# Another order in front of the first attention turn of a decoder layer

## The chip, the cores and the metric

The kernel runs on one core of a Trainium2 chip. The metric is the device time of one execution in microseconds (us), as the median over runs. The engines are named as the profile names them: PE (TensorE, with PEld for its weight loads), DVE (VectorE), ACT (ScalarE), POOL (GpSimd) and SP (the engine that issues most transfers). All data are float32.

## The reference, cut to what matters

One decoder layer over two sequences of 1024 tokens with 256 features: a linear attention with two decays per head, a cross attention to 154 context rows, and a mixture of eight experts (two per token) with a shared expert, each on a normalised input and added to the residual.

```python
x = x + linear_attn(layernorm(x), w_qkv, w_out, alpha, beta)
x = x + cross_attn(layernorm(x), ctx, weights, mask, Wq, bq, Wk, bk, Wv, bv, Wo, bo)
x = x + experts(layernorm(x), ...)

def linear_attn(x, w_qkv, w_out, alpha, beta):      # 16 heads of 16
    q, k, v = split(x @ w_qkv, 3)
    q, k = elu(q) + 1, elu(k) + 1
    for d in (sigmoid(alpha), sigmoid(beta)):       # one decay per head
        run_kv, run_k = scan(d, k * v), scan(d, k)  # out[t] = d * out[t-1] + in[t]
        den = max(sum(q * run_k over the head), 1e-6)
        outs.append(q * run_kv / den)
    return concat(outs) @ w_out

def cross_attn(x, ctx, weights, mask, ...):         # 16 heads of 64
    q, k, v = x @ Wq + bq, ctx @ Wk + bk, ctx @ Wv + bv
    att = softmax(where(mask, -inf, (q @ k.T) / 8 * weights))
    return (att @ v) @ Wo + bo
```

## The kernel before

Tokens are cut into four blocks of 512 (`BLK`), two per sequence; a block is four tiles of 128 tokens. The cross attention runs in 64 "turns" (block, group of four heads, tile). A turn takes `score` (L1007, PE), `weigh` (L1016, DVE), `hide` (L1028, DVE), `power` (L1037, ACT), `divide` (L1044 on DVE, L1045 and L1048 on POOL) and, three turns later, transposes (L961) and the product with the values. Behind the turns come the router, the shared expert and the routed experts.

In front of the first turn stands a prologue, which is written out by hand: inside `manual_schedule` every engine gets its instructions in the order in which Python emits them, and each engine works its own queue strictly in that order, waiting on semaphores. Later work (the linear attention of blocks 1 to 3, the rest of the keys and values, the norms of blocks 2 and 3) is cut into generators, `linear_rest`, `rest_of_kv` and `other_norms`, of which every turn takes one piece (`ahead`).

The prologue does these things, each with its lines:

- `load_x`, and the weight loads on SP's queue in the order alpha_beta, w_qkv, x of block 1, ctxT, bk, Wk, Wv, w_out, x of blocks 2 and 3, and then the rest.
- `layernorm_early` for blocks 0 and 1: statistics on DVE (L186, L187), the reciprocal root on POOL (L190, L191), the normalised rows on DVE for block 0 (L199) and on ACT for block 1 (L204), eight transposes on PE (L212), and copies out of PSUM (L216 on DVE, L218 on ACT).
- `make_decay`: the decays of alpha and beta, spread over the partitions by four small matmuls (L358), copied out on DVE (L362).
- The linear attention of block 0, for two chunks c of 128 features: `make` projects k or q (`project`, L451), ACT takes an exponential and a Relu of it (L463, L464), and DVE joins them (the "map", L466). `make_v` multiplies v into k (L473). `scan_k` and `scan_kv` are decayed prefix sums on DVE (L478, two decays f per chunk), of keys and of keys times values. `times_q` (L490) and `num_q` (L497) multiply by q. `sum_rows` sums per head on PE with `sel` (L505), and DVE takes the reciprocal (L513, L514). `spread` brings it back over the partitions with `selT` (L524), DVE multiplies (L533), and `result` multiplies by w_out (L543) and adds to x (L548).
- `keys(o)` makes one eighth of the keys of the cross attention (L378, and L382 on ACT), `vals` half of the values of a sequence (L390, L395), `rests` the values of the last 26 context rows (L402, L406).
- The norm of the queries of block 0 in two halves (`layernorm`, L228 to L256), `add_bo` on POOL (L608), and the first three pieces of block 1 (`second`).

The maps and the multiplications by PSUM results are put off in two lists, `mapped` and `later`, and issued together by `take_later`. PSUM has three tiles `mm` of one bank, one `tp`, and two tiles `sc` of two banks, which the scores use; in the prologue every product goes to an `mm` tile. A float32 matmul shows as two records in the trace, so a projection has four records.

Before, the prologue makes keys 0 to 3 and the values of sequence 0, and `rest_of_kv` takes keys 4 and 5 in the first turn and keys 6 and 7 in the fourth.

Of the kernel before, what the change touches and what calls it, by code (L numbers as in the profile page):

```python
# [8 lines left out]
F32 = mybir.dt.float32  # L9
# [16 lines left out]
def tile_decoder_layer(  # L26
# [81 lines left out]
    def load_x(blk, parts=1):  # L108
        b, r = divmod(blk, NBB)
        n = TPB // parts  # L110
        for i in range(parts):
# [3 lines left out]
                in_=x[b, q0 : q0 + n * P, :].rearrange("(t p) d -> p t d", p=P),  # L115
            )

    load_x(0, 2)

    Wq_sb = xconst.tile([P, ND, NO * P], F32, tag="Wq", name="Wq_sb")  # L120
# [53 lines left out]
    for e in range(E):  # L174
        nc.gpsimd.memset(rank[:, e : e + 1], float(E - e))

    def layernorm_early(blk, lnT):

        src = xr[blk]
        first = blk == 0  # L180
        st = small.tile([P, TPB, 6], F32, tag="st", name="st")
        mv = small.tile([P, TPB, 2], F32, tag="mv", name="mv")
        rstd = small.tile([P, TPB], F32, tag="rstd", name="rstd")
        nmr = small.tile([P, TPB], F32, tag="nmr", name="nmr")
        for t in range(TPB):
            nc.vector.bn_stats(st[:, t, :], src[:, t, :])  # L186
            nc.vector.bn_aggr(mv[:, t, :], st[:, t, :])  # L187
            if t == 1:
                yield
        nc.gpsimd.tensor_scalar(rstd, mv[:, :, 1], LN_EPS, None, ALU.add)  # L190
        nc.gpsimd.tensor_tensor(rstd, rstd, half[:, 0:1].to_broadcast([P, TPB]), ALU.pow)  # L191
        if not first:
            nc.gpsimd.tensor_tensor(nmr, mv[:, :, 0], rstd, ALU.mult)
            nc.gpsimd.tensor_scalar(nmr, nmr, -1.0, None, ALU.mult)
        yield
        xn = xnp.tile([P, TPB, DX], F32, tag="xn", name="xn")
        for t in range(TPB):
            if first:
                nc.vector.tensor_scalar(  # L199
                    xn[:, t, :D], src[:, t, :], mv[:, t, 0:1], rstd[:, t : t + 1],  # L200
                    ALU.subtract, ALU.mult,
                )
            else:
                nc.scalar.activation(  # L204
                    xn[:, t, :D], src[:, t, :], AF.Identity,
                    bias=nmr[:, t : t + 1], scale=rstd[:, t : t + 1],
                )
        yield
        for c in range(ND):
            tp = mm_tile()  # L210
            for t in range(TPB):
                nc.tensor.transpose(  # L212
                    tp[:, t * P : (t + 1) * P], xn[:, t, c * P : (c + 1) * P], ident
                )
            if first and c == 0:
                nc.vector.tensor_copy(lnT[:, c, :], tp)  # L216
            else:
                nc.scalar.copy(lnT[:, c, :], tp)  # L218
        yield

    def layernorm(blk, lnT, xn, t0=0, nt=TPB):
# [62 lines left out]
    wk = weights.enter_context(tc.tile_pool(name="wk", bufs=1, side="right"))  # L284


    ab = kw.tile([NR, 1], F32, tag="ab", name="ab")
    nc.sync.dma_start(out=ab, in_=alpha_beta)
    wqkv_sb = kw.tile([P, ND, 3 * D], F32, tag="wqkv", name="wqkv_sb")
    nc.sync.dma_start(out=wqkv_sb, in_=w_qkv.rearrange("(c p) o -> p c o", p=P))  # L290
    load_x(1)
    ctxT_sb = wk.tile([P, ND, B * SK], F32, tag="ctxT", name="ctxT_sb")
    nc.sync.dma_start(out=ctxT_sb, in_=ctxT.rearrange("(c p) k -> p c k", p=P))
    nc.sync.dma_start(out=bk_sb, in_=bk)
    Wk_sb = wk.tile([P, ND, NO * P], F32, tag="Wk", name="Wk_sb")
    nc.sync.dma_start(out=Wk_sb, in_=Wk.rearrange("(c p) o -> p c o", p=P))
    Wv_sb = wk.tile([P, ND, H * DK], F32, tag="Wv", name="Wv_sb")
    nc.sync.dma_start(out=Wv_sb, in_=Wv.rearrange("(c p) o -> p c o", p=P))
    wout_sb = kw.tile([P, 2 * ND, D], F32, tag="wout", name="wout_sb")
    nc.sync.dma_start(out=wout_sb, in_=w_out.rearrange("(c p) o -> p c o", p=P))  # L300
# [66 lines left out]
    nbk = wk.tile([P, NO], F32, tag="nbk", name="nbk")  # L367

    def prepare_kv():
        for b in range(B):  # L370
            nc.gpsimd.tensor_copy(ctx2[:, :, b, :], ctxT_sb[:, :, b * SK + P : (b + 1) * SK])
        nc.gpsimd.memset(vr_sb, 0.0)
        nc.gpsimd.tensor_scalar(nbk, bk_sb, -1.0 / (MASKED * float(DK) ** 0.5), None, ALU.mult)

    def keys(o):
        ps = mm_tile()
        for c in range(ND):
            nc.tensor.matmul(  # L378
                ps[:, : B * SK], lhsT=Wk_sb[:, c, o * P : (o + 1) * P],
                rhs=ctxT_sb[:, c, :], start=(c == 0), stop=(c == ND - 1),  # L380
            )
        nc.scalar.activation(  # L382
            kT[:, o, :], ps[:, : B * SK], AF.Identity, bias=nbk[:, o : o + 1],
            scale=-1.0 / (MASKED * float(DK) ** 0.5),
        )
# [50 lines left out]
    class Linear:  # L436
# [8 lines left out]
            self.num = lp.tile([P, NX, BLK], F32, tag="num", name="num", bufs=1)  # L445
            self.rden = lp.tile([P, TQ], F32, tag="rden", name="rden", bufs=1)

        def project(self, o):
            ps = mm_tile()
            for c in range(ND):  # L450
                nc.tensor.matmul(  # L451
                    ps, lhsT=wqkv_sb[:, c, o * P : (o + 1) * P], rhs=lnTa[self.blk][:, c, :],
                    start=(c == 0), stop=(c == ND - 1),
                )
            return ps
# [10 lines left out]
                lambda: nc.vector.scalar_tensor_tensor(dst, e, 1.0, dst, ALU.min, ALU.add)  # L466
            )

        def make_v(self, c):

            ps = self.project(2 * ND + c)
            k = self.k[c]
            later.append(lambda: nc.vector.tensor_tensor(k, ps, k, ALU.mult))  # L473

# [40 lines left out]

            later.append(take)

        def spread(self, half):

            js = (2 * half, 2 * half + 1)  # L520
            pss = {j: mm_tile() for j in js}
            for xi in range(NX):
                for j in js:
                    nc.tensor.matmul(  # L524
                        pss[j][:, xi * TQ : (xi + 1) * TQ],
                        lhsT=selT[rows_of(j), xi * P : (xi + 1) * P], rhs=self.rden[rows_of(j), :],
                        start=True, stop=True,
                    )
            for j in js:
                n = self.num[:, :, j * TQ : (j + 1) * TQ]  # L530
                ps = pss[j].rearrange("p (x q) -> p x q", x=NX)
                later.append(
                    lambda n=n, ps=ps: nc.vector.tensor_tensor(n, ps, n, ALU.mult)  # L533
                )

        def result(self, t0):

            ps = mm_tile()
            po = ps.rearrange("p (t d) -> p t d", d=D)
            for i in range(2):  # L540
                at = (t0 + i) * P
# [49 lines left out]
    def take_later():  # L591
        for take in mapped + later:
            take()
        mapped.clear()
        later.clear()
# [27 lines left out]
    with region:  # L623
        L = [Linear(blk) for blk in range(NBLK)]
        a = L[0]
        second = L[1].pieces()
        dk = make_decay()
        make_selT(0)
        next(ln[0])
        next(ln[0])  # L630
        next(dk)
        next(ln[0])
        next(ln[1])
        next(ln[0])
        next(dk, None)
        next(ln[1])
        next(ln[1])
        make_sel()
        prepare_kv()
        a.make("k", 0)  # L640
        take_later()
        a.begin()
        a.make("q", 0)
        a.scan_k(0, 0)
        a.make_v(0)
        a.scan_k(0, 1)
        take_later()
        a.make("k", 1)
        a.make("q", 1)
        for f in range(2):  # L650
            a.scan_kv(0, f)
        next(ln[1])
        take_later()
        for f in range(2):
            a.times_q(0, f)
        a.make_v(1)
        for f in range(2):
            a.scan_k(1, f)
        keys(0)
        keys(1)  # L660
        take_later()
        for j in range(1, TG):
            make_selT(j)
        nc.gpsimd.memset(zero, 0.0)
        for f in range(2):
            a.times_q(1, f)
        vals(0, 0)
        a.sum_rows()
        for f in range(2):
            a.num_q(0, f)  # L670
        take_later()
        for f in range(2):
            a.scan_kv(1, f)
        rests(0)
        a.spread(0)
        for f in range(2):
            a.num_q(1, f)
        take_later()
        rests(512)
        a.spread(1)  # L680
        take_later()
        keys(2)
        next(ln[2])
        next(ln[2])
        a.result(0)
        a.result(2)
        half_0, half_2 = later
        later.clear()
        next(second)
        half_0()  # L690
        lnTq[0] = lnT_tile(0)
        xq = xnp.tile([P, TPB, DX], F32, tag="xn", name="xn")
        nq0 = [layernorm(0, lnTq[0], xq, t, 2) for t in (0, 2)]
        next(nq0[0])
        half_2()
        next(nq0[1])
        next(nq0[0])
        take_later()
        keys(3)
        next(second)  # L700
        for _ in range(ND):
            next(nq0[0])
        next(nq0[1])
        take_later()
        for _ in range(ND):
            next(nq0[1])
        add_bo(0)
        vals(0, 512)
        next(second)


    HL = HID - (NHC - 1) * P
# [195 lines left out]
    with bctx:  # L908
# [197 lines left out]

        def rest_of_kv():

            keys(4)
            keys(5)  # L1110
            yield
            for n0 in (0, 512):
                vals(1, n0)
                yield
            keys(6)
            keys(7)
            yield
            bias_rows()
            yield
# [463 lines left out]
```

## Time and profile before

| what | value |
|---|---|
| runs | 646.98, 645.94, 643.26 us; median 645.94 |
| profiled execution | 646.79 us, its span 645.1 us |
| mean granted clock of PE | 0.984 |
| busy: PE, DVE, ACT, POOL | 605.5, 431.9, 296.8, 244.0 us |
| first matmul record | 8.19 us |
| first turn (first L1016 on DVE) | 70.35 us |
| last turn (last L1016) | 385.0 us |

The span runs from the first to the last instruction of the one profiled execution. A row of the timeline has the start in us, the length in us, the engine, the line, the operation, the tiles written and read, their shapes, how many instructions are merged, and in brackets how long the engine had been idle before it and what ended that. A row of the windows has a stretch, its length, the busy time of PE, PEld, DVE, ACT and POOL with the number of records, the granted clock, the share of the transfer engines and GB/s.

### The profile page before, as it was taken

The page shows a single profiled execution, that of the slowest core. Times are in us where ns is not written, and L with a number is a line of the kernel's source. Part 1 is how long each engine was busy: PE and PEld are TensorE (multiplying, and loading weights), DVE is VectorE, ACT ScalarE, POOL GpSimd, SP SyncE. Part 2 cuts the span into 40 slices and gives each one's busy share as a digit, 9 for nine tenths or more (in the row PEclk, how much of TensorE's full clock was granted, in tenths as well). Part 3 has the DMA queues.
Part 4 walks back from the last instruction along what each step waited for, and adds up shares of the span by engine and source line. Part 5 has one row for each costly group of instructions (what it writes and reads, how often), then busy time and mean ns, then how long its engine had stood idle before and what let it go on. Part 6 is the DMA issues. An engine that isn't in the chain of part 4 may idle for free. (4 is left out here: it accounts for less than half of the span.)

```text
span 645.1 us, 10259 instructions
## 1 busy us (share of the span) xinstructions
PE 605.5 (94%) x3024; PEld 393.3 (61%) x3024; DVE 431.9 (67%) x1379; ACT 296.8 (46%) x894; POOL 244.0 (38%) x375
## 2 busy tenths in 40 slices
PE   4898999999999998999899989899899999999897
PEld 3354466555577545777467654667477777777644
DVE  4887595689844899656984694248456655556557
ACT  1512577677545766437785586122222222222221
POOL 4712043332322423218642582515344444444200
PEclk9988999999999999899999989979999999999999
DMA  8800468977976474254453330895112221212055
GB/s 302 231 15 2 113 164 211 235 186 176 204 176 157 116 172 94 56 136 124 107 133 74 88 82 1 283 344 224 49 57 60 65 65 60 67 59 65 34 203 205
DMA packets 111411, 83.79 MB, mean 130 GB/s; under 512 B 41858, under 2 KB 104819, under 8 KB 111228
## 3 DMA queue, kind: packets, MB, share of 16 engines
q1 hardware_dynamic: 106364, 69.42, 41.1%
q0 software_dynamic: 4992, 13.71, 6.6%
q8 instruction: 26, 0.43, 0.3%
q14 instruction: 29, 0.24, 0.1%
HBM read 54.90 MB, written 27.98 MB: 128 GB/s over the span
## 5 line engine op out<-in xcount | busy, mean ns | idle before, releaser
L1045 POOL TENSOR_TENSOR s<-s,sums 128x512 f32<-128x512 f32 x64 | 66.9, 1045 | 177.6 <-DVE sums L1044 168.1
L1037 ACT ACTIVATE s<-s,nm 128x154 f32<-128x154 f32 x256 | 104.8, 416 | 6.3 <-DVE nm L1028 6.1
L1028 DVE CUSTOM_DVE_ANT_0 s<-s,mk 128x154 f32<-128x154 f32 x256 | 93.2, 418 | 1.2
L1379 PE MATMUL sc<-W_sb,xT 128*128 x288 | 91.2, 460 | 0.1
L1426 POOL DMA_INDIRECT y_tab<-y,to x36 | 35.5, 986 | 81.7 <-DVE to_f L1405 58.8
L1379 PEld LDWEIGHTS sc<-W_sb,xT 128*128 128x128 f32 x288 | 51.9, 190 | 23.2 <-issue 0.4
L1385 DVE TENSOR_TENSOR ea<-sc,b 128x704 f32<-128x704 f32 x36 | 32.1, 891 | 50.5 <-PE sc L1379 48.7
L941 PE MATMUL mm<-lnT,Wq_sb 128*128 128x512 f32 x128 | 60.7, 598 | 0.6 <-ACT oT L997 0.6
L1058 PE MATMUL mm<-Wo_sb,oT 128*128 128x256 f32 x256 | 60.2, 391 | 0.0
L962 ACT COPY pT<-tp 128x512 f32<-128x512 f32 x64 | 36.9, 576 | 43.3 <-PE tp L961 42.7
L1058 PEld LDWEIGHTS mm<-Wo_sb,oT 128*128 128x128 f32 x256 | 49.9, 198 | 9.5 <-issue 2.2
L1007 PEld LDWEIGHTS sc<-kT,qT 64*128 64x128 f32 x512 | 37.3, 190 | 30.1 <-issue 12.0
L1007 PE MATMUL sc<-kT,qT 64*128 64x154 f32 x512 | 51.5, 320 | 4.3 <-DVE s L1016 3.7
L1016 DVE TENSOR_TENSOR s<-sc,fs 128x616 f32<-128x616 f32 x64 | 50.0, 781 | 6.3 <-PE sc L1007 6.3
L1037 ACT ACTIVATION_READ_ACCUMULATOR s<-s,nm 128x1 f32 x256 | 49.4, 193 | 0.0
L451 PE MATMUL mm<-lnT,wqkv_sb 128*128 128x512 f32 x96 | 46.8, 624 | 0.0
L961 PE MATMUL tp<-ident,s 128*128 128x128 f32 x256 | 42.7, 290 | 4.4 <-POOL s L1045 3.9
L873 PE MATMUL sc<-lnT,Ws_sb 128*128 128x512 f32 (+1 forms) x96 | 42.9, 594 | 0.4 <-PEq L1510 0.4
L1417 PE MATMUL mm<-W_sb,hT 128*128 x168 | 41.1, 380 | 1.5 <-DVE to_f L1405 1.5
L821 POOL DMA_INDIRECT x_tab<-xn,slot x32 | 32.3, 1010 | 25.1 <-issue 14.9
L1344 POOL DMA_INDIRECT xb<-x_tab,rows_i x36 | 34.7, 965 | 12.3 <-issue 9.4
L961 PEld LDWEIGHTS tp<-ident,s 128*128 128x128 f32 x256 | 27.7, 144 | 16.6 <-issue 9.2
(222 smaller groups left out, 1016.6 us busy)
## 6 DMA issues: line engine op xcount, KB each, us to landing
fs<-in_fside SPq DMA_DIRECT2D x64, 308.0 KB
x_tab<-book SPq DMA_DIRECT2D x32, 516.0 KB
W_sb<-in_w SPq DMA_DIRECT2D x16, 352.0 KB
mk<-in_mask SPq DMA_DIRECT2D x64, 77.0 KB
W_sb<-y_tab SPq DMA_DIRECT2D x16, 256.0 KB
b<-b_tab SPq DMA_DIRECT2D x1, 2816.0 KB
W_sb<-in_w SPq DMA_DIRECT2D x8, 256.0 KB
out<-xr SPq DMA_DIRECT2D x16, 128.0 KB
```

The source lines that it names most:

```text
L451: nc.tensor.matmul(ps, lhsT=wqkv_sb[:, c, o * P : (o + 1) * P], rhs=lnTa[self.blk][:, c, :], start=(c == 0), stop=(c == ND - 1),)
L873: nc.tensor.matmul(ps[:hn, :], lhsT=Ws_sb[:, at : at + hn], rhs=lnT[:, d, :], start=(d == 0), stop=(d == ND - 1),)
L941: nc.tensor.matmul(ps, lhsT=Wq_sb[:, c, o * P : (o + 1) * P], rhs=lnTq[self.blk][:, c, :], start=(c == 0), stop=(c == ND - 1),)
L961: nc.tensor.transpose(tp[:, j * P : (j + 1) * P], s[:, j, :P], ident)
L1007: nc.tensor.matmul(sc[:, par, pair * SK : (pair + 1) * SK], lhsT=gr.qT[pair][rows, t * P : (t + 1) * P], rhs=kT[rows, 2 * gr.g + pair, gr. ...
L1016: begun = nc.vector.tensor_tensor(s[:, :, :SK].rearrange("p (pair par) k -> p par pair k", par=2), sc[:, :, : 2 * SK].rearrange("p par (pa ...
L1028: nc.vector.tensor_tensor_reduce(s[:, j, :], s[:, j, :], gr.mk[t][:, j, :], MASKED, FLOOR, ALU.add, ALU.min, nm[:, j : j + 1],)
L1037: nc.scalar.activation(s[:, j, :SK], s[:, j, :SK], AF.Exp, bias=nm[:, j : j + 1], scale=-1.0, accum_out=sums[:, j : j + 1],)
L1045: nc.gpsimd.tensor_tensor(s[:, :, :P], s[:, :, :P], sums.unsqueeze(2).to_broadcast([P, HG, P]), ALU.mult)
L1058: nc.tensor.matmul(ps[:, :D], lhsT=oTs[blk][o][:, t * P : (t + 1) * P], rhs=Wo_sb[0][:, o, :], start=(o == 0), stop=(o == NO - 1),)
L1379: nc.tensor.matmul(ab[:, j, :HID], lhsT=self.xT[:, d, :], rhs=W_sb[:, bass.ds(ev, 1), at : at + HID].rearrange("p a h -> p (a h)"), start= ...
L1417: nc.tensor.matmul(po[:, :D], lhsT=self.hT[:kn, c, :], rhs=W_sb[:kn, bass.ds(self.ev, 1), O2 + c * D : O2 + (c + 1) * D].rearrange("p a d ...
```

## The change

The order of the prologue is written anew; no arithmetic is added or taken away but a few small instructions.

- The norm of block 0 has a function of its own, `first_norm`: the reciprocal root is taken for two tiles at a time, tile 2 is normalised on ACT and the others on DVE, and the transposes go in two halves.
- bk, ctxT and the first quarter of Wk are loaded in front of w_qkv, and `keys(0)` is the first work on PE; its copy on ACT is put off until after the norm (`keys` now returns the copy as a function). alpha_beta is loaded from ACT's queue. `nbk` is made on POOL in front of the norm's root.
- The decay matmuls come after the first projection, the norm of block 1 on ACT after the four maps' inputs.
- Sums of keys go in front of the values: both `scan_k`, `times_q` and `sum_rows` come before `scan_kv`.
- `make_v`, `spread` and `result` of block 0 use tiles of the `sc` pool instead of `mm` tiles.
- keys 1 to 5 and both halves of the values of sequence 0 are made before the first result, and `rest_of_kv` keeps keys 6 and 7 only.
- The statistics of block 2 stand in front of the spread multiplications, and the second half of the query norm stands in front of the maps and scans of block 1.

```diff
+    ab = const.tile([2 * H, 1], F32, tag="ab", name="ab")
+    nc.scalar.dma_start(out=ab, in_=alpha_beta)
     load_x(0, 2)
...
+    def first_norm(lnT):
+        src = xr[0]
...
+        for h in range(2):
+            some = slice(2 * h, 2 * h + 2)
+            for t in (2 * h, 2 * h + 1):
+                nc.vector.bn_stats(st[:, t, :], src[:, t, :])
+                nc.vector.bn_aggr(mv[:, t, :], st[:, t, :])
+            nc.gpsimd.tensor_scalar(rstd[:, some], mv[:, some, 1], LN_EPS, None, ALU.add)
+            nc.gpsimd.tensor_tensor(
+                rstd[:, some], rstd[:, some], half[:, 0:1].to_broadcast([P, 2]), ALU.pow
+            )
+        for t in range(TPB):
...
+        tps = [mm_tile() for _ in range(ND)]
+        for h in range(2):
+            for c in range(ND):
+                for t in (2 * h, 2 * h + 1):
+                    nc.tensor.transpose(
+                        tps[c][:, t * P : (t + 1) * P], xn[:, t, c * P : (c + 1) * P], ident
+                    )
+        nc.vector.tensor_copy(lnT[:, 0, :], tps[0])
+        nc.scalar.copy(lnT[:, 1, :], tps[1])
...
-    ab = kw.tile([NR, 1], F32, tag="ab", name="ab")
-    nc.sync.dma_start(out=ab, in_=alpha_beta)
...
+    nc.sync.dma_start(out=bk_sb, in_=bk)
+    nc.sync.dma_start(out=ctxT_sb, in_=ctxT.rearrange("(c p) k -> p c k", p=P))
+    nc.sync.dma_start(out=Wk_sb[:, :, some_k], in_=Wk_rows[:, :, some_k])
     nc.sync.dma_start(out=wqkv_sb, in_=w_qkv.rearrange("(c p) o -> p c o", p=P))
     load_x(1)
...
+    nc.sync.dma_start(out=Wk_sb[:, :, rest_k], in_=Wk_rows[:, :, rest_k])
     nc.sync.dma_start(out=Wv_sb, in_=Wv.rearrange("(c p) o -> p c o", p=P))
...
     with region:
...
+        first = first_norm(lnTa[0])
+        do(kv)
+        take_k = keys(0)
+        do(first, dk, first)
+        take_k()
+        do(ln[1], ln[1])
         a.make("k", 0)
-        take_later()
+        do(dk)
+        on_dve()
         a.begin()
         a.make("q", 0)
         a.scan_k(0, 0)
-        a.make_v(0)
         a.scan_k(0, 1)
-        take_later()
+        on_dve()
+        make_sel()
+        do(kv)
+        two = sc_tile()
+        a.make_v(0, two[:, 0, :])
         a.make("k", 1)
-        a.make("q", 1)
-        for f in range(2):
-            a.scan_kv(0, f)
-        next(ln[1])
-        take_later()
         for f in range(2):
             a.times_q(0, f)
-        a.make_v(1)
+        a.make("q", 1)
+        on_dve()
+        do(ln[1])
         for f in range(2):
             a.scan_k(1, f)
-        keys(0)
-        keys(1)
-        take_later()
+        keys(1)()
+        keys(2)()
+        do(ln[1])
+        for f in range(2):
+            a.times_q(1, f)
+        a.make_v(1, two[:, 1, :])
+        keys(3)()
...
         a.sum_rows()
         for f in range(2):
-            a.num_q(0, f)
-        take_later()
+            a.scan_kv(0, f)
+        on_dve()
+        vals(0, 0)
+        vals(0, 512)
+        rests(0)
         for f in range(2):
             a.scan_kv(1, f)
-        rests(0)
-        a.spread(0)
+        for f in range(2):
+            a.num_q(0, f)
+        keys(4)()
+        a.spread(0, sc_tile())
         for f in range(2):
             a.num_q(1, f)
-        take_later()
+        do(ln[2], ln[2])
+        keys(5)()
         rests(512)
-        a.spread(1)
-        take_later()
-        keys(2)
-        next(ln[2])
-        next(ln[2])
-        a.result(0)
-        a.result(2)
-        half_0, half_2 = later
-        later.clear()
-        next(second)
-        half_0()
+        on_dve()
+        a.spread(1, sc_tile())
+        two = sc_tile()
+        a.result(0, two[:, 0, :])
+        half_0 = later.pop()
+        on_dve()
+        a.result(2, two[:, 1, :])
+        half_2 = later.pop()
...
+        half_0()
+        do(nq0[0], second)
         half_2()
-        next(nq0[1])
-        next(nq0[0])
-        take_later()
-        keys(3)
-        next(second)
...
+        do(nq0[0], nq0[1])
+        do(nq0[0], nq0[0], nq0[1])
+        on_dve()
+        do(second)
+        do(nq0[1], nq0[1])
+        on_dve()
         add_bo(0)
-        vals(0, 512)
-        next(second)
+        do(second)
...
         def rest_of_kv():
-            keys(4)
-            keys(5)
+            keys(6)()
             yield
             for n0 in (0, 512):
                 vals(1, n0)
                 yield
-            keys(6)
-            keys(7)
+            keys(7)()
             yield
```

## The prediction

> **What bounds the kernel now.** I read the page first, for the whole:
>
> ```profile
> PE 605.5 (94%) x3024; PEld 393.3 (61%) x3024; DVE 431.9 (67%) x1379; ACT 296.8 (46%) x894; POOL 244.0 (38%) x375
> ```
>
> TensorE sets the pace of the whole, but its idle time is not spread evenly. The change touches what lies in front of the first turn, so I read the timeline of the first 84 us next, and in it who came late at each hand-over. The first is the start of VectorE's long chain:
>
> ```profile
> 14.93 0.34 PEld L451 LDWEIGHTS mm<-lnT,wqkv_sb 128*128 128x128 f32 x1 [0.52 <-issue]
> 15.78 0.34 PEld L451 LDWEIGHTS mm<-lnT,wqkv_sb 128*128 128x128 f32 x1 [0.52 <-issue]
> 16.48 0.19 PEld L451 LDWEIGHTS mm<-lnT,wqkv_sb 128*128 128x128 f32 x1 [0.36 <-issue]
> 16.91 0.19 PEld L451 LDWEIGHTS mm<-lnT,wqkv_sb 128*128 128x128 f32 x1 [0.24 <-issue]
> ...
> 15.64 2.07 ACT L204 ACTIVATE xn<-xr,nmr,rstd 128x256 f32<-128x256 f32 x4 [4.54 <-POOL nmr L194]
> 17.62 0.57 ACT L463 ACTIVATE e<-mm 128x512 f32<-128x512 f32 x1
> 18.71 0.69 DVE L466 SCALAR_TENSOR_TENSOR k<-e,k 128x512 f32<-128x512 f32 x1 [5.16 <-ACT k L464]
> ```
>
> A projection is four of these loads. Until 16 us they stand 0.85 us apart, afterwards 0.43: the first projection takes 3.4 us, later ones 1.7. It is done near 15.7, but ScalarE is then at the norm of block 1 until 17.6, so VectorE's first map of keys starts at 18.71. From there VectorE has no idle time worth a line up to 41.6. The next hand-overs:
>
> ```profile
> 42.75 1.29 DVE L533 TENSOR_TENSOR num<-mm,num 128x512 f32<-128x512 f32 x2 [1.12 <-PE mm L524]
> 43.97 7.07 PE L543 MATMUL mm<-wout_sb,num 128*128 128x256 f32 x32
> 58.61 0.71 DVE L240 TENSOR_SCALAR xn<-xr,mv,rstd 128x256 f32<-128x256 f32 x2
> 59.14 0.78 PE L249 MATMUL mm<-ident,xn 128*128 128x128 f32 x4 [1.48 <-DVE xn L240]
> 59.40 2.35 POOL L608 TENSOR_TENSOR xr<-xr,bo_bc 128x1024 f32<-128x1024 f32 x1 [5.16 <-DVE xn L240]
> 59.95 4.05 DVE L478 TENSOR_TENSOR_SCAN num<-decay,state,k 128x512 f32<-128x512 f32 x2
> 70.35 0.80 DVE L1016 TENSOR_TENSOR s<-sc,fs 128x616 f32<-128x616 f32 x1 [6.35 <-PE sc L1007]
> ```
>
> The results of block 0 (L543) start at 43.97. The second half of the query norm (L240) stands on VectorE behind two scans, until 58.61; then TensorE does values (L390), one more projection and both query projections before the scores, and the first turn (L1016) starts at 70.35 after VectorE has waited 6.35 us. Last, the windows of the first turns, to see which engine takes over:
>
> ```profile
> 72.00:76.00 4.00, 4.00 (x13) 2.24 (x12) 3.97 (x8) 2.19 (x4) 0.00 (x0) 1.00 0.93 229
> 76.00:80.00 4.00, 4.00 (x18) 1.99 (x17) 3.99 (x12) 3.48 (x11) 0.00 (x0) 1.00 0.74 185
> 92.00:96.00 4.00, 3.99 (x24) 2.22 (x23) 3.97 (x12) 3.58 (x11) 3.17 (x6) 1.00 0.67 144
> 96.00:100.00 4.00, 2.71 (x21) 1.51 (x20) 3.59 (x14) 3.79 (x13) 2.33 (x3) 1.00 0.79 171
> ```
>
> The columns after the length are TensorE, its loads, VectorE, ScalarE, GpSimd. VectorE (3.97, 3.99, 3.97 of 4) is full in these turns; TensorE falls to 2.71 at 96 to 100. So what the change moves of the first turn's start is worth its whole amount, and TensorE work taken out of these turns is worth little.
>
> **The change, stage by stage.** The span is 645.1 us, the profiled execution 646.79 (1.69 around it), 0.85 above the median 645.94. I follow three marks: T0, VectorE's first map of keys (18.71 now); S, the first result matmul (43.97); W, the first turn (70.35).
>
> *Up to T0.* bk, ctxT and a quarter of Wk go in front of w_qkv on SP's queue: 0.004, 0.315 and 0.262 MB. Now x of block 1 stands at 1.83 MB in the queue and lands at 10.12, when VectorE's statistics stop waiting. The windows show 137, 286 and 397 GB/s in the first three stretches of 4 us, so 1.83 MB are through by 8.4 and the landing comes 1.7 later. By the same count the quarter of Wk (1.11 MB) is through by 6.0 and lands near 7.7, w_qkv (1.89 MB) near 10.2, x of block 1 (2.41 MB) near 11.5. keys(0) now heads TensorE's queue: it holds the transposes from 7.7 on for four records of 0.28, twice that at the slow pace, 2.2 us, to 9.9; now they start at 8.19. What feeds them is in time: the norm's rows by halves need GpSimd's 0.23 and 0.73 (the L234, L235 rows for two tiles) after the statistics; nbk, put in front of them on GpSimd, waits for bk, third on its queue as alpha_beta is now, which landed at 5.19, so it delays them by about 0.5. Last rows at 8.7, hidden behind keys(0). Eight transposes, 2.29: 12.2. The copies take 0.59: the first projection starts at 12.2 to 12.7, as now (12.20); w_qkv is there, and 2 us late would cost nothing. The four small decay matmuls (1.86 now) move behind it. At the slow pace it ends at 15.7, ScalarE's two passes (1.06) at 16.8, decay at 17.4: T0 = 17.4. At the full pace T0 = 15.8. I take the middle, 16.6. ScalarE no longer has the norm of block 1 in front (it follows q of chunk 1). Gain 2.1, bounds 1.3 and 2.9. What else moves on the queues costs nothing here: alpha_beta goes to ScalarE's queue in front of its table load (an issue of 0.47 beside 1.28) and is needed only by the decay matmuls; the rest of Wk (cumulated 3.2 MB, landing near 14 by the same count) and Wv are asked for after 20; on GpSimd sel, ctx2 and the other selT rows run in the order of now, until 28, and the sums need them at T0 + 12.7 = 29, so only a delay of more than a us there would be seen.
>
> [...] The row: eight us after its first transpose at 8.19, and 3.9 after 12.20, TensorE doubles its rate; the granted clock reads 1.00 throughout, so the page's clock column does not show this one. [...]
>
> *T0 to S.* VectorE's work from 18.71 to the end of the first spread multiplications at 41.63 is 22.9 us without idle, and it stays (sums of keys first only reorders it). Added in front of the spread: statistics of block 2, eight instructions from 43.95 to 46.2, 2.3. One new wait: TensorE does q, v, k, q of chunks 0 and 1 after decay, 4 x 1.71 = 6.8, and ScalarE 1.06: the second map of q is ready at T0 + 7.7. VectorE is there after map 0.73, scans 2.8, map 0.75, products 1.28, map 0.75 = T0 + 6.3. 1.4 lost; queued behind it are all its scans. TensorE's sums, values, rests, keys and both spreads (13 to 14 us) fit beside VectorE's 12.1 after the sums; the tiles of the sc pool take away the wait of 1.12. S = T0 + 22.9 + 2.3 + 1.4 = T0 + 26.6 = 43.2. Gain here -1.3 (now 25.3), bounds 0 and -3, the last if the slow pace returns for 4 us as it does from 33 us now.
>
> *S to W.* Results 7.1, second half added to 7.8, rows of the first half 8.5, statistics 9.7, GpSimd 1.2, rows of the second half at 11.7: in front of the scans now, where they stood behind (58.61 is S + 14.6). Then two maps 1.4, two scans 2.45; GpSimd's add_bo (2.35) runs beside them, and the row at 59.95 shows what that does: two scans in 4.05, so 1.6 more. v is multiplied by S + 17.8. The instruction order shows the second query projection waiting for VectorE, on the buffer that this multiplication frees: 17.9 + 1.7 = 19.6, ScalarE 0.69, scores and hand-over 0.6: W = S + 21.0. VectorE's two scans end at 20.3, just under. Now it is 26.4. keys(2), keys(3) and vals(0, 512), which took TensorE 1.3, 1.2 and 3.4 at the slow pace, are done before S. Gain 5.4, bounds 3.9 (another 1.5 of contention) and 6.9 (no wait for the buffer).
>
> *Turns.* W = 16.6 + 26.6 + 21.0 = 64.2, 6.15 earlier. keys(4) and keys(5) leave turn 0 (keys(6) comes instead), and keys(7) is left alone later: 2 x 1.12 of TensorE. Of that I count 0.7, the wait of VectorE for ScalarE at 80.71 (0.72), whose passes stood behind the two kT copies. If all 2.24 count, 1.5 more; if nothing, 0.7 less.
>
> Sum: 2.1 - 1.3 + 5.4 + 0.7 = 6.9. 646.79 - 6.9 = 639.9; for the median 0.85 less, 639.0.
>
> **Rivals.**
> - More: the array is fast from 12.5 on (0.8 more), no wait for the second q (1.4), no wait for the buffer (1.5), all keys count (1.5): all four make 12.1, 633.8, two or three of them 635 to 637. For it: TensorE is at work without a gap from 7.7 on. Against it: each needs its own good luck. 0.20.
> - Less: T0 = 17.4 and a slow stretch of TensorE before the sums (3 us more), more contention in front of W (1.5): 6.9 - 0.8 - 1.7 - 1.5 = 2.9, so 643. For it: the slow pace returned at 33 and at 60 us. 0.14.
> - [...] 0.08.
> - The forecast, 637 to 642: 0.58. That the order is not what the change says is excluded by the instruction order.
>
> **Numbers.** A measurement of this kernel tells about 0.5% from no change: 3.2 us, so 642.7 is the border. Faster 0.79 (forecast, "more", a little of "less"), same 0.13, slower 0.08. The range 633.5 to 643.5 takes in "more" and most of "less".
>
> **What would show it.** T0 near 16.6 and W near 64 in the timeline; no 6.35 us of VectorE idle before L1016's successor; a wait of about 1.4 before the second map of q; add_bo beside slow scans; turns of block 0 shifted whole. A W at 64 with the time unchanged would refute the claim that the shift is carried through; a W past 68 the sum itself.

## The result and the profile after

The changed kernel takes 641.33 us (median of 21 runs, 638.82 to 647.59) where the kernel before took 646.15 beside it (median of 21): a ratio of 0.9942, 95% interval [0.9916, 0.9968]. That is faster by 0.6% (the two medians alone give 0.75%), inside the predicted range, and 2.3 us above the predicted time. Its profiled execution took 644.08 us (span 642.3), 2.75 more than its own median; what differs in such executions is told in experiment 1.

The marks of the prediction, read from the timeline of the changed kernel, stand in these lines (start, length, engine, line, operation; in brackets the idle time before and what ended it):

```profile
7.86 2.39 PE L421 MATMUL mm<-ctxT_sb,Wk_sb 128*128 128x308 f32 x4 [7.86 <-DMA Wk_sb<-in_Wk]
10.04 1.56 PE L222 MATMUL mm<-ident,xn 128*128 128x128 f32 x8
12.16 1.98 PE L494 MATMUL mm<-lnT,wqkv_sb 128*128 128x512 f32 x4 [0.56 <-DVE lnT L225]
15.30 0.69 DVE L509 SCALAR_TENSOR_TENSOR k<-e,k 128x512 f32<-128x512 f32 x1
21.63 0.69 DVE L509 SCALAR_TENSOR_TENSOR k<-e,k 128x512 f32<-128x512 f32 x1 [0.91 <-ACT k L507]
23.34 1.00 DVE L509 SCALAR_TENSOR_TENSOR q<-e,q 128x512 f32<-128x512 f32 x1 [1.02 <-ACT q L507]
42.52 7.14 PE L586 MATMUL sc<-wout_sb,num 128*128 128x256 f32 x32 [0.39 <-PE sc L567]
49.70 0.69 DVE L591 TENSOR_TENSOR xr<-sc,xr 128x512 f32<-128x512 f32 x1 [6.09 <-PE sc L586]
55.88 0.74 DVE L280 TENSOR_SCALAR xn<-xr,mv,rstd 128x256 f32<-128x256 f32 x2 [1.23 <-POOL rstd L275]
56.70 3.32 POOL L651 TENSOR_TENSOR xr<-xr,bo_bc 128x1024 f32<-128x1024 f32 x1 [0.85 <-DVE xn L280]
57.74 4.54 DVE L521 TENSOR_TENSOR_SCAN rks<-decay,state,k 128x512 f32<-128x512 f32 x2
63.14 1.98 PE L993 MATMUL mm<-lnT,Wq_sb 128*128 128x512 f32 x4 [1.97 <-DVE k L516]
66.48 0.80 DVE L1068 TENSOR_TENSOR s<-sc,fs 128x616 f32<-128x616 f32 x1 [0.90 <-PE sc L1059]
```

What to see: the first projection (12.16) takes 1.98 us with its loads 0.43 apart, which is full pace, and T0 is 15.30. The two maps of chunk 1 wait 0.91 + 1.02. S is 42.52. Then comes the surprise: VectorE idles 6.09 us, and its first addition (L591) begins only when all 7.14 us of result matmuls are done, although it needs half of them. Everything behind it is late by that: the normalised rows, the scans (4.54 for two, with GpSimd's addition of bo beside them), and the second query projection, which waits 1.97 for a buffer. W is 66.48 instead of 64.2.

In the first turns VectorE is as full as before, and TensorE falls below it at 88 to 92. The columns are length, TensorE, its loads, VectorE, ScalarE, GpSimd, granted clock, transfers:

```profile
68.00:72.00 4.00, 4.00 (x17) 2.01 (x17) 4.00 (x9) 2.06 (x4) 0.00 (x0) 1.00 0.89 225
72.00:76.00 4.00, 4.00 (x15) 1.93 (x12) 3.96 (x13) 4.00 (x14) 0.00 (x0) 1.00 0.72 170
88.00:92.00 4.00, 2.89 (x20) 1.82 (x19) 3.97 (x13) 3.86 (x10) 2.88 (x6) 1.00 0.77 191
```

Turn by turn the changed kernel is ahead by 3.87 (first turn), 4.68 (third), some 5.16 (from the seventh on), 5.43 (from the 46th on) and 5.42 (last, 379.59 against 385.01). At the end only 2.8 of it is left.

### The profile page after: what moved, and what is told of

It is laid out like the page before. It is cut to its first block, busy times and chain, and to the rows that moved or that the text cites. A ratio compares the mean times of both kernels' runs of the same rounds, so it can differ in the third digit from the quotient of the medians.

```text
span 642.3 us, 10262 instructions
## 1 busy us (share of the span) xinstructions
PE 605.3 (94%) x3024; PEld 392.1 (61%) x3024; DVE 432.0 (67%) x1380; ACT 296.9 (46%) x895; POOL 248.3 (39%) x377
## 5 line engine op out<-in xcount | busy, mean ns | idle before, releaser
L1429 PE MATMUL sc<-W_sb,xT 128*128 x288 | 92.9, 466 | 0.2 <-issue 0.2
L1110 PE MATMUL mm<-Wo_sb,oT 128*128 128x256 f32 x256 | 58.7, 384 | 0.0
L494 PE MATMUL mm<-lnT,wqkv_sb 128*128 128x512 f32 x88 | 41.4, 601 | 1.0 <-DVE lnT L225 0.6
```

The costliest lines, as they stand in the source:

```text
L494: nc.tensor.matmul(ps, lhsT=wqkv_sb[:, c, o * P : (o + 1) * P], rhs=lnTa[self.blk][:, c, :], start=(c == 0), stop=(c == ND - 1),)
L1110: nc.tensor.matmul(ps[:, :D], lhsT=oTs[blk][o][:, t * P : (t + 1) * P], rhs=Wo_sb[0][:, o, :], start=(o == 0), stop=(o == NO - 1),)
L1429: nc.tensor.matmul(ab[:, j, :HID], lhsT=self.xT[:, d, :], rhs=W_sb[:, bass.ds(ev, 1), at : at + HID].rearrange("p a h -> p (a h)"), start= ...
```

## The experiments

The traces in one table (us, one profiled execution each): T0, S - T0, the first turn W, W - T0, the last turn, and what follows it. Ten runs of the changed kernel lay between 635.6 and 642.3 us (experiment 1), so the time of a kernel with one run says little; there the marks are compared. "Half clock" stands for stretches in which the windows show a granted clock near 0.5.

| kernel | T0 | S - T0 | W | W - T0 | last turn | last turn to end |
|---|---|---|---|---|---|---|
| before | 18.71 | 25.26 | 70.35 | 51.64 | 385.01 | 260.1 |
| changed | 15.30 | 27.22 | 66.48 | 51.18 | 379.59 | 262.7 |
| changed, again | 16.28 | 26.77 | 67.96 | 51.68 | 381.38 | 257.6 |
| own tile | 16.48 | 26.75 | 64.69 | 48.21 | 377.58 | 257.4 |
| own tile, again | 15.77 | 27.21 | 64.41 | 48.64 | 379.22 | 257.6 |
| keys(0) late | 14.67 | 27.23 | 66.66 | 51.99 | 380.04 | 257.2 |
| keys 4, 5 back | 16.14 | 27.21 | 69.61 | 53.47 | 385.69 | 257.3 |
| values first | 15.55 | 28.83 | 68.36 | 52.81 | 381.40 | 260.7 |
| bo on TensorE | 15.36 | 27.20 | 64.43 | 49.07 | 379.44 | 260.6 |
| own tile, bo on TensorE | 16.05 | 26.76 | 64.09 | 48.04 | 380.58 | 257.3 |
| own tile, keys(0) late | 15.87 | 30.30 | 67.62 | 51.75 | 382.58 | 256.6 |
| bo of all blocks on TensorE, own tile | 16.30 | 26.75 | 64.33 | 48.03 | 385.89 | 262.4 |
| old norm, keys(0) late | 15.88 | 27.25 | 67.03 | 51.15 | 382.02 | 257.5 |

**1. The changed kernel again.** No edit.

> The changed kernel once more, with a profile of its own. Theory: the first turn starts near 66.5 us and the last near 379.6 us (5.4 earlier than before), since nothing up to there depends on chance; what lies behind the last turn (260.1 us before, 262.7 after in the first profiles) depends on where TensorE's slow stretches fall, and comes out between 257 and 264. Rival: the 2.6 us lost behind the last turn belong to the new order; then it is 262.7 again, within 0.5.

Measured: 641.35 us (median of 10), ratio 0.9925 [0.9889, 0.996]; 257.6 us from the last turn to the end instead of 262.7. The loss behind the turns was chance, as expected. What it is shows in the windows behind the last turns, first of the first execution, then of this one:

```profile
376.00:380.00 4.00, 4.00 (x24) 3.67 (x23) 3.96 (x20) 3.76 (x14) 2.28 (x5) 0.54 0.01 4
380.00:384.00 4.00, 4.00 (x17) 3.12 (x19) 2.34 (x12) 1.91 (x9) 2.28 (x4) 0.50 0.00 0
384.00:388.00 4.00, 4.00 (x14) 1.02 (x11) 0.00 (x0) 0.14 (x1) 0.84 (x3) 0.68 0.00 0
```

```profile
376.00:380.00 4.00, 3.21 (x30) 2.88 (x30) 3.93 (x12) 3.77 (x17) 3.17 (x5) 1.00 0.11 37
380.00:384.00 4.00, 4.00 (x26) 2.36 (x28) 3.93 (x21) 3.25 (x13) 2.15 (x4) 1.00 0.00 0
384.00:388.00 4.00, 4.00 (x15) 1.83 (x12) 0.86 (x6) 3.23 (x12) 1.88 (x3) 1.00 0.01 2
```

The granted clock (0.54, 0.50, 0.68 against 1.00) is what differs: 4 x (0.46 + 0.50 + 0.32) = 5.1 us of clock, some of it just ahead of the last turn at 379.59. Of the traces of the table, the five with 260.1 to 262.7 us behind the last turn all show a half clock between 376 and 393, and none of those with 256.6 to 257.6 does. The two go together, but the sizes do not match one for one: experiments 6 and 7 lost the same 5.1 us of clock there and ended at 260.7 and 260.6. In front of the half clock TensorE idles for much the same time in both executions:

```profile
375.00 0.66 PE L1013 MATMUL tp<-ident,s 128*128 128x128 f32 x4 [1.80 <-POOL s L1097]
```

```profile
376.80 0.66 PE L1013 MATMUL tp<-ident,s 128*128 128x128 f32 x4 [1.95 <-POOL s L1097]
```

After the gap of 1.80 us the clock fell, after the gap of 1.95 it did not. The length of the gap does not decide it: at this place TensorE idles 1.79 or 1.80 us in eleven of the thirteen traces, and the clock fell in five of them (the kernel before, the changed kernel, experiments 6, 7 and 9) and not in six (both executions of experiment 2, experiments 3, 5, 8 and 10). But W came 1.48 later here, so the front has chance in it too. T0 is 0.98 later, of which 0.45 was made up by S. After a wait of TensorE for the same buffer (1.98 us, 1.97 in the first execution) the clock fell this time, from about 65 to 68.4, and W came another 0.95 later after S.

**2. The second half of the results in a tile of its own.** The one edit for the addition that waited:

```diff
-        a.result(2, two[:, 1, :])
+        a.result(2, sc_tile()[:, 0, :])
```

> Only the second half of block 0's result goes to a PSUM tile of its own instead of the second bank of the first half's tile. Theory: the addition of the first half waited for the second half's matmuls because both write one tile; now it runs 3.5 us earlier (near 46.2 instead of 49.7), VectorE's wait of 6.1 falls to 2.6, and the first turn starts near 64.1 instead of 66.5, with the whole time 2.4 lower. Rival: TensorE's projections and the wait for a buffer in front of the second query projection set the first turn anyway; then it moves by less than 0.5.

```profile
43.23 7.17 PE L586 MATMUL sc<-wout_sb,num 128*128 128x256 f32 x32
46.99 0.69 DVE L591 TENSOR_TENSOR xr<-sc,xr 128x512 f32<-128x512 f32 x1 [2.35 <-PE sc L586]
50.45 0.69 DVE L591 TENSOR_TENSOR xr<-sc,xr 128x512 f32<-128x512 f32 x1 [1.56 <-PE sc L586]
59.56 3.77 PE L993 MATMUL mm<-lnT,Wq_sb 128*128 128x512 f32 x8
64.69 0.80 DVE L1068 TENSOR_TENSOR s<-sc,fs 128x616 f32<-128x616 f32 x1 [0.90 <-PE sc L1059]
```

Now the first addition is 3.76 behind S, and the second follows the second half directly. The two query projections (59.56) run without a gap, so the wait of 1.97 is gone too. S to W is 21.46 (21.0 was predicted for the change). The time is 636.61 us (median of 4), ratio 0.985 [0.9799, 0.9901]. Run again beside other kernels:

> The kernel with the second half of the results in a tile of its own, run again beside the one before it. Theory: first half's addition 3.6 to 3.8 behind the first result matmul, first turn 48.2 behind the first map of keys, time 0.985 of the kernel before as in the first run, 2 to 3 us less than the changed kernel. Rival (the first run had luck with the clock behind the turns): ratio 0.992 or more, no better than the changed kernel.

Measured: first addition at S + 3.73 (42.98, 46.71), S to W 21.43, 636.32 us (median of 4), ratio 0.9854 [0.9816, 0.9892]. W - T0 was 48.64, 0.4 above the theory's, all of it in front of S. The wait for the whole tile was the cause: in the changed kernel the addition is issued behind the matmuls of both halves, and both halves write one tile. This version beats the kernel before by both intervals; against the changed kernel its median is 4.7 us lower in the same round (641.35), of which 2.5 to 3.5 are W - T0, and the rest is not explained.

**3. keys(0) behind the first projections.**

```diff
         do(kv)
-        take_k = keys(0)
         do(first, dk, first)
-        take_k()
...
         a.make("q", 1)
         on_dve()
+        keys(0)()
```

> keys(0) is taken from the head of TensorE's queue and made together with keys 1 and 2; the loads stay as in the changed kernel. Theory: keys(0) is what brings TensorE to full pace before the first projection; without it the transposes start earlier (near 7.4) but the first projection runs at half pace, 3.4 us from about 10.6 to 14.0, and VectorE's first map starts near 16, later than the 15.30 of the changed kernel. Rival: the pace comes with time or with the transposes; then the projection takes 1.7 and the map starts near 14.4, earlier than now.

Measured: 638.93 us in one run. The transposes start at 7.10 instead of 10.04, the first projection at 10.42, at half pace, and T0 is 14.67:

```profile
10.42 3.09 PE L494 MATMUL mm<-lnT,wqkv_sb 128*128 128x512 f32 x4 [0.49 <-DMA wqkv_sb<-in_w_qkv]
11.41 0.34 PEld L494 LDWEIGHTS mm<-lnT,wqkv_sb 128*128 128x128 f32 x1 [0.52 <-issue]
12.26 0.34 PEld L494 LDWEIGHTS mm<-lnT,wqkv_sb 128*128 128x128 f32 x1 [0.52 <-issue]
```

The loads stand 0.85 apart until about 13. So the slow pace comes back when keys(0) is taken from the front, but the earlier start pays for it: against the changed kernel's first execution keys(0) in front bought nothing; T0 is 0.6 earlier without it.

**4. Both of these edits.**

> The second half of the results in a tile of its own, and keys(0) behind the first projections. Theory (each step carries through to the first turn, TensorE has no gap between the first projection and the scores, so what counts is when it starts and what it has to do): first map of keys 14.7 (15.3 to 16.5 with keys(0) in front), first turn 48.2 later as with the own tile alone, 62.9, time 1 to 1.5 less than with the own tile alone. Rival (keys(0) is TensorE work that has to be done anyway; put behind, it pushes all that follows by its 1.2): first map 14.7, first turn 49.4 later, 64.1, and the time the same as with the own tile alone within 0.5.

Measured: 638.16 us (median of 4), ratio 0.9891 [0.9857, 0.9924]; T0 15.87, W 67.62. Neither the theory nor the rival: this time the half pace lasted through three projections, to 21.8 us (their times were 3.75, 3.78 and 3.17), and W - T0 was 51.75. So keys(0) late looks like the worse bet: without it in front TensorE came to full pace at 13.2, 14.7 and 21.8 us in three executions (experiments 3, 10 and 4; 16.2 in the kernel before), with it at 11.0 to 14.3 in all nine, read from the spacing of the loads. It is not shown in the time: three executions are few, T0 was no later in them (14.67 to 15.88 against 15.3 to 16.5), and the intervals of this ratio and of the own tile alone overlap.

**5. keys 4 and 5 back in the turns.**

```diff
-        keys(4)()
         a.spread(0, sc_tile())
...
-        keys(5)()
...
-            keys(6)()
+            keys(4)()
+            keys(5)()
...
+            keys(6)()
             keys(7)()
```

> keys 4 and 5 go back into the first turn, and keys 6 and 7 into the fourth, as before. Theory: the lead over the kernel before grows by 0.8 at the third turn and by 0.45 at the seventh because these keys are gone; with them back the first turn stays at 66.5 and the lead stays at its 3.9 there up to the last turn, which then starts near 381. Rival: the lead grows for other reasons, and the last turn starts at 379.6 as now.

Measured: 644.77 us in one run. S - T0 is the same (27.21), but W - T0 is 53.47, 1.8 to 2.3 us more than in the two executions of the changed kernel, and from there to the last turn it takes 316.08 against 313.11 and 313.42: against the first execution 1.12 more up to the third turn, 0.45 up to the seventh, 1.6 up to the tenth. The 1.6 are a half clock from 100.8 to 104.3, after 1.28 us of idle TensorE between 96 and 100; the first two are near the 0.8 and 0.45 of the theory. The part in front has a face in the windows:

```profile
40.00:42.00 2.00, 0.49 (x10) 0.30 (x6) 1.86 (x9) 0.02 (x1) 0.00 (x0) 1.00 0.06 13
42.00:44.00 2.00, 0.65 (x2) 0.59 (x3) 2.00 (x5) 0.00 (x0) 1.58 (x4) 0.69 0.13 27
44.00:46.00 2.00, 2.00 (x6) 1.60 (x5) 0.44 (x1) 0.00 (x0) 0.13 (x1) 0.50 0.13 27
46.00:48.00 2.00, 2.00 (x10) 1.75 (x9) 0.00 (x0) 0.00 (x0) 0.00 (x0) 0.95 0.14 31
```

Without the two keys TensorE idles from 40.5 to 43.3, the clock falls to half for about 3.4 us, and that hits the result matmuls: the first addition comes 8.58 behind S (43.35, 51.93) instead of 7.18. A second half clock, from 66.6 on, took the rest of the 2.3; the second execution of the changed kernel had such a one too. In the same way the kernel before had 0.35 of 2 us busy at 30 to 32 and half a clock at 34 to 36. The gap here was 2.86 us and the clock fell. But the length of a gap alone does not tell it: for the gaps of 1.80 to 1.98 us of experiment 1 the clock fell in two cases and did not in two, and in experiment 4, where TensorE was idle for 3.13 of the 4 us from 412 to 416, it stayed at 1.00.

**6. Sums of values in front again.** The running sums of values of chunk 0 go back in front of the sums of keys of chunk 1:

```diff
+        for f in range(2):
+            a.scan_kv(0, f)
         for f in range(2):
             a.scan_k(1, f)
...
-        for f in range(2):
-            a.scan_kv(0, f)
```

> The running sums of values of chunk 0 stand in front of the sums of keys of chunk 1 again, as before the change; all else is the changed kernel. Theory (the new place keeps TensorE at work): the sums of keys are ready 2.6 us later (two scans of about 1.3), what TensorE has in front of them lasts no longer than now, so TensorE stands idle for some 2 us near 28 to 31 and its clock then falls to half for about 3.4 us, as in the kernel before at 33 to 36; the spread and the first result come 1.1 to 2.8 us later than in the changed kernel, measured from the first map of keys. First result minus first map of keys 28.3 to 30.0 (27.2 in the changed kernel), first turn later by the same 1.1 to 2.8. Rival 1 (only a reordering of VectorE's work, which has no idle time there): 27.2 and no half clock. Rival 2: the whole 2.6 shows with the clock untouched, 29.8.

Measured: S - T0 28.83 (27.2 and 26.8 in the changed kernel), W 1.1 to 1.6 later after T0, 643.84 us in one run. The place of the sums is worth 1.6 to 2.1 up to S in this execution; the smaller figure at W is against the execution that lost 0.95 to a half clock behind S. It came by the route of the theory without its clock: TensorE was busy 0.43 of 2 us at 30 to 32 and kept its clock; VectorE then waits for the second spread, which TensorE reaches late:

```profile
44.49 1.29 DVE L576 TENSOR_TENSOR num<-sc,num 128x512 f32<-128x512 f32 x2 [2.39 <-PE sc L567]
```

**7. bo of block 0 added by TensorE.** `add_bo(0)` is left out, and in `project_out` of block 0 one matmul with a single row comes first:

```diff
-        add_bo(0)
...
+            if blk == 0:
+                nc.tensor.matmul(
+                    ps[:, :D], lhsT=ones_sb[0:1, :], rhs=bo_bc[0:1, :], start=True, stop=False
+                )
```

> The changed kernel without GpSimd's addition of bo to block 0 (2.35 to 3.3 us of GpSimd); TensorE adds bo in the output projection of block 0 instead, one small matmul for each of four tiles, some 50 us and more later. The output is the same function. Theory (that addition slows the two scans beside it): the pair of scans takes 2.45 instead of 4.54, the multiplication of v comes 2.1 earlier, the second query projection no longer waits 1.97 for its buffer, and first turn minus first map of keys falls from 51.2 to 51.7 (two runs of the changed kernel) to 49.3. Rival 1 (the scans are slow there for another reason, such as their start value): the pair stays at 4.5 and the turn where it is. Rival 2 (the scans get fast, but TensorE's own work in front of the scores is as late): 4.54 falls to 2.45 and the turn comes less than 0.7 earlier.

```profile
57.78 2.45 DVE L521 TENSOR_TENSOR_SCAN rks<-decay,state,k 128x512 f32<-128x512 f32 x2
64.43 0.80 DVE L1067 TENSOR_TENSOR s<-sc,fs 128x616 f32<-128x616 f32 x1 [0.90 <-PE sc L1058]
```

The two scans take 2.45 instead of 4.54, and W - T0 is 49.07: the theory, to a quarter of a us. But the 2.05 us gained at the first turn (against the changed kernel) stand at 1.25 at the 23rd turn, 0.43 at the 25th, and turn into a loss of 0.39 at the 27th and 1.2 at the 30th: 0.82 for each of the four small matmuls, which are in the trace as

```profile
162.73 0.69 PE L1109 MATMUL mm<-bo_bc,ones_sb 1*128 1x256 f32 x2
```

So in those turns TensorE is the bound (it is busy without idle from 160 to 200), and each of the four put there cost its whole time. At the last turn the two kernels are level again (0.15), because the changed kernel's execution has a half clock from 253.4 to 256.9 that this one has not. 641.72 us in one run.

**8. Own tile and bo on TensorE.**

> The second half of the results in a tile of its own and block 0's bo added by TensorE, both. Theory: with the own tile TensorE waits only 0.73 for the buffer, so the second edit is worth 0.8 of the first turn here, not 2.0: first turn minus first map of keys 47.4 (48.2 with the own tile alone), time 635.8. Rival 1 (the two add up): 46.2 and 634.6. Rival 2 (TensorE is without a gap from the results to the scores by then, nothing is left): 48.2 and 636.6.

Measured: W - T0 48.04 against 48.21 with the own tile alone, so rival 2 for the front. The time is 640.54 (median of 10), ratio 0.9935 [0.9899, 0.9971], by the ratios some 5 us more than with the own tile alone. Of that 3.3 are the four small matmuls, by the turns as in experiment 7; the expectation had not counted them. The other 2 are not explained. The wait of 0.73 on which the theory counted was one of TensorE's weight loads only: its two query projections took 3.77 us without a gap with the own tile alone and take 3.60 here, which is the 0.17 gained. VectorE now waits longer in front of the first turn, and that is the point:

```profile
64.09 0.80 DVE L1067 TENSOR_TENSOR s<-sc,fs 128x616 f32<-128x616 f32 x1 [2.83 <-PE sc L1058]
```

It waits 2.83 where it waited 0.90 with the own tile alone: its scans are faster by 2.1, but TensorE works through projections and queries with hardly a gap, and the scores come no earlier.

**9. bo of all four blocks on TensorE.** 

> As the kernel with both edits, and bo of blocks 1, 2 and 3 is added by TensorE too. Theory: in the turns the scans beside GpSimd's addition are slowed by 2 us for each block, but after the first turns TensorE is as full as VectorE, so of 3 x 2 us at most a third shows: 0 to 2 us faster than the kernel with both, 634 to 636. Rival 1 (VectorE bounds all those turns): 6 us faster, 630. Rival 2 (TensorE bounds them, and 12 small matmuls of some 0.2 us are added): 2 us slower, 638.

Measured: 648.04 us (median of 10), ratio 1.0046 [1.0009, 1.0082], 7.5 more than the kernel of experiment 8 for 12 more small matmuls. Rival 2 had the sign and was wrong in size: 0.2 us a matmul was put where 0.6 was paid on the mean, less than the 0.82 of the turns of block 0.

**10. The old norm.** On the kernel with keys(0) late, where nothing stands in front of the norm: the inverse deviation of four tiles at once, and all rows on VectorE.

> The kernel with keys(0) behind the first projections, and in it the first norm as before the change: the inverse deviation of all four tiles at once on GpSimd, all four rows on VectorE. To be compared with the kernel with keys(0) late, whose copy of the turned rows is at 9.55, whose first projection starts at 10.42 (it waits 0.49 for w_qkv) and whose first map of keys is at 14.67. Theory (the norm over two engines buys nothing that is not hidden): the rows come near 7.5 to 9.2, the transposes end near 9.7, the copy comes 0.2 to 0.6 later, and of that the wait for w_qkv hides up to 0.5: first map of keys 14.6 to 14.9. Rival (the norm is what set the start): the transposes come 1.1 later as in the kernel before (8.19 against 7.10), first map of keys 15.6 to 15.8.

Measured: T0 15.88 against 14.67, as the rival has it, but not all by its route. The transposes start at 8.29 (7.10), the copy at 10.18 (9.55), the first projection at 10.92 (10.42), and that projection takes 3.78 instead of 3.09, because the full pace came at 14.7 instead of 13.2. The norm over two engines is worth 0.5 to 0.6 when it is in front of everything; the other 0.7 is the pace, which differs as much between two executions of one kernel. In the changed kernel the transposes start at 10.04, behind keys(0), and the old norm's last rows end at 9.60 here, so there the norm is not on the path.

## Why the prediction was right, and where it was not

The predicted gain was 6.9 and the time 639.0; the medians differ by 4.8. By its steps, in the profiled execution:

- **T0**: 16.6 (15.8 to 17.4) predicted, 15.30 measured; 15.3 to 16.5, on the mean 15.9, over nine executions with keys(0) in front. The landings were close (keys(0) began at 7.86, 7.7 predicted). A first projection at half pace to its end would have made 17.4, and no execution showed that: in four of nine the first projection ran at full pace from its start, in five it changed pace on the way. What brings TensorE from half to full pace no run shows; with keys(0) in front it came between 11.0 and 14.3 us. Nor was T0 always 15.8; the middle of the two was a size put too high.
- **T0 to S**: 26.6 predicted, 27.22 and 26.77 measured in the two executions. The new wait of VectorE was 1.93, not 1.4. The prediction gave the sums' new place no gain of its own ("only reorders it"). It was worth 1.6 to 2.1 (experiment 6): the 22.9 us of VectorE without idle, which the prediction kept, hold only with it.
- **S to W**: this is the step that failed. 21.0 predicted, 23.96 measured. The prediction put the rows of the first half at S + 8.5 and those of the second at S + 11.7, with the first half added as soon as its matmuls are done. Both halves write the two banks of one `sc` tile, the addition waited for the last write to the tile, and so came at S + 7.2; the first half's rows came at S + 10.3 and the second half's at S + 13.4. Taking the shared tile away alone gave 21.46 and 21.43. The rest of this step was sized well: two scans beside GpSimd 4.54 (4.05 in the row it was taken from), and the wait of the second query projection for a buffer was there, 1.97.
- **Turns**: +0.7 predicted from the wait at the third turn, where 0.81 came; 0.45 and 0.25 more came later, 1.55 in all. The claim that TensorE work taken out is worth little holds only for the first turns: from the 23rd on each small matmul of 0.69 cost 0.82.
- **Behind the turns**: nothing was predicted and 2.6 were lost in the profiled execution: 256.6 to 257.6 or 260.1 to 262.7, whichever kernel, and the longer ones are those with a half clock after one gap of TensorE (experiment 1).

That makes 3.41 - 1.96 + 2.42 + 1.55 = 5.42 at the last turn; 3.63 in the second execution of the same kernel, whose T0 and clock were less lucky. That the time still lay 2.3 us from the predicted one is in part luck: T0 and the turns came out 2.2 us better than their terms, T0 to S and S to W 3.6 us worse.

**The rivals.** A slower kernel (0.08) did not come: the ratio was 0.9942, and TensorE was at full pace from 14.3 us on at the latest, but for the half clocks told of. "Less" put a slow stretch before the sums; one came in the second execution, but between S and W, and cost 0.95. "More" had T0 = 15.8 and all keys counting, and both came near, but paid only for part of the shared tile.

What stays open: what decides whether a gap of TensorE costs the clock. Gaps of one length at one place did both (1.80 us, five times of eleven), and no run varied such a gap alone.

## What to carry to other kernels

When an operation is read as "starts when its half is done", look up which tile both halves live in: here the addition waited for the tile's last writer (it began 7.2 us behind the first matmul, and 3.7 to 3.8 with a tile for each half), and the second tile cost nothing here and brought the first turn some 3 us forward (2.5 to 3.5, measured from T0). Work that only fills an engine's idle time in a prologue can still be worth its place: without keys 4 and 5 a gap of 2.86 us opened and the clock fell, in the one execution there is. Judge a filler by the gap that it covers. And settle per stage which engine is full: the same 3 us addition was worth 2 us of VectorE in front of the first turn, nothing once TensorE was the bound there (W - T0 48.04 against 48.21), and a loss of some 3.3 us when moved as four small matmuls into turns where TensorE had no idle time.

## What the runs showed of the hardware

- A gap of TensorE of 1.80 and one of 1.98 us were followed by 10 and 3.5 us of half clock; gaps of 1.95 and 1.97 at the same places in the other execution were not. Over all traces the gap of 1.80 at that place was followed by a half clock in five of eleven, 1.28 us of idle between 96 and 100 were followed by one (experiment 5), and 3.13 us of idle between 412 and 416 were not (experiment 4). The half clock behind the turns is the largest difference between the two traces of the changed kernel, whose ten runs of experiment 1 lie between 635.6 and 642.3 us.
- Two scans with two inputs took 4.54 beside GpSimd's addition (two inputs, 3.32) and 2.45 without it (experiment 7); the price was 2.1 of the addition's 3.3.
- A matmul with one row of 256 columns (two records) took 0.69 us, 0.34 a record, where the 16 records of 128 x 256 behind it took 3.72, 0.23 each: the matmul on one partition was no cheaper here than those on 128.
